# A state space layer and a windowed attention layer on one core: dividing the softmax numerators on GpSimd, and moving work across the border of the two layers

## The chip, the cores and the metric

The program runs on one core of a Trainium2 chip. The metric is the device time of one execution in microseconds (us), from the first to the last instruction of the core. The engines of the core are named as in its profile: PE (TensorE, matrix products and transposes; PEld is its weight load), DVE (VectorE), ACT (ScalarE), POOL (GpSimd) and SP (SyncE, which here only issues DMA transfers). All arithmetic is in fp32.

## The reference, cut to what matters

Two residual layers follow each other on `x` of shape (4, 384, 64, 64). Each is preceded by a group norm over 32 groups of 12 channels. Layer 0 is a state space layer (a scan over 4096 positions); the change touches only its surroundings. Layer 1 is attention of 12 heads of 32 channels over a 7 by 7 window around each pixel.

```python
def _L1_conv_ref(x, w_qkv, b_qkv, w_proj, b_proj, rel_bias):
    ...                                           # q, k, v: 1x1 products; edges of k and v repeated
    logits = jnp.stack([jnp.einsum('bnchw,bnchw->bnhw', q, k_pad[..., di:di + H, dj:dj + W])
                        for di in range(ws) for dj in range(ws)], axis=-1)
    logits = logits + rel_bias.reshape(nh, ws * ws)[None, :, None, None, :]
    attn = jax.nn.softmax(logits, axis=-1)
    v_win = ...                                   # the 49 shifted copies of v
    out = jnp.einsum('bnhwk,bnkchw->bnchw', attn, v_win).reshape(B, C, H, W)
    out = jnp.einsum('oc,bchw->bohw', w_proj, out) + b_proj[None, :, None, None]
    return out

x = x + _L0_conv_ref(_gn(x), ...)                 # state space layer
x = x + _L1_conv_ref(_gn(x), ...)                 # attention
```

## The kernel before

Layer 0 gives its instructions in the order in which the engines run them. In layer 1 the order on each engine is chosen when the program is built: an instruction may come before others that stand ahead of it in the code, once its inputs are there. Each engine then works through its own list strictly in that order, and waits where an input or a buffer is missing.

Layer 1 works on stripes of 8 rows of an image (32 stripes). A stripe has 4 blocks of 8 by 16 pixels, and a block has 3 groups of 4 heads. One group of one block is called a **step** here: 12 steps in a stripe, 384 in all. A step computes scores of 128 pixels against a common neighbourhood of 14 by 22 = 308 positions, with a bias table that masks what is outside of each pixel's own window.

```python
def scores(b, s, bl, m, blk):
    sg = w2.tile([P, 4, NK], F32, tag="sg", ...)             # 2 buffers
    mx = w2.tile([P, 4], F32, tag="mx", ...)
    for hh in range(4):
        lg = bank(ps_l, "lg")                                # 4 PSUM banks
        nc.tensor.matmul(lg[:, :NK], ...q..., ...k..., start=True, stop=True)       # L887
        nc.vector.tensor_tensor_reduce(                                            # L893
            sg[:, hh, :], lg[:, :NK], bias[:, 4 * m + hh, :], -1.0, BIG,
            ALU.add, ALU.min, mx[:, hh : hh + 1])
        act(sg[:, hh, :], sg[:, hh, :], AF.Exp, scale=-1.0, bias=mx[:, hh : hh + 1],
            accum_out=blk["sum"][:, 4 * m + hh : 4 * m + hh + 1])                   # L96
    return sg

def weighted(m, sg, blk):                     # numerators turned, so that positions are partitions
    ta = []
    for pair in range(2):
        pt = bank(ps_t, "pt")                                # 2 PSUM banks
        ...nc.tensor.transpose(pt[...], sg[...], ident)      # 4 of them, L912
        t = w2.tile([P, 4, P], F32, tag="ta", bufs=4)
        nc.vector.tensor_copy(...t..., pt[: KN[0], :])       # L917
        ta.append(t)
    pt = bank(ps_t, "pt")
    ...nc.tensor.transpose(pt[...], sg[:, hh, KOFF[2] :], ident)   # 4 of them, L923
    tb = w2.tile([P, 4, P], F32, tag="tb")
    nc.scalar.copy(...tb..., pt[: KN[2], :])                 # L927
    return ta, tb

def attended(m, ta, tb, blk):                 # L935: products with the window of v, 12 of them
    ...

def block_end(bl, blk, aT):                   # once in three steps
    rs = w2.tile([P, NH], F32, tag="rsum")
    nc.vector.reciprocal(rs, blk["sum"])                                           # L944
    rb = w2.tile([P, NH, HD], F32, tag="rb")
    nc.gpsimd.tensor_copy(rb, rs.unsqueeze(2).broadcast_to([P, NH, HD]))           # L946
    pr = bank(ps, "mm")                                      # the only bank of this pool
    for m in range(NJ):
        nc.tensor.transpose(pr[...], rb[...], ident)                               # L949
    rt = w2.tile([P, NJ, P], F32, tag="rt")
    nc.scalar.copy(..rt.., pr[:, : NJ * P])                                        # L954
    nc.vector.tensor_tensor(aT[...], blk["o"][...], ..rt.., ALU.mult)              # L955
```

The loop gives, in each step, the scores of this step, the product with v of the step before last, the transposes of the last step, and one part of `projected` (keys, values and queries of the next stripe) or of `stripe_end` (output projection of the last stripe). Both use the one bank of pool `ps`.

```python
for m in range(NJ):
    sg = scores(b, s, bl, m, blk)
    if turned is not None:
        attend()                              # attended(), and block_end() after the third group
    turned = None
    if pending is not None:
        pm, psg, pblk, *rest = pending
        turned = (pm, *weighted(pm, psg, pblk), pblk, *rest)
    pending = (m, sg, blk, bl, b, s, aT)
    if ends and next(ends[0], None) is None:
        ends.pop()
    elif not ends:
        next(ahead, None)                     # a part of projected(next stripe)
```

At the border of the layers, layer 1 first loads the bias table, then turns the channel statistics of all four images into group statistics (`group_stats`: eight small parts that depend on each other, with matrix products, DVE copies and ACT roots), and then projects the first stripe through the single bank of `ps`. The weights of layer 1 (`w_qkv`, `w_pj`) were loaded at the start of the program, and 18 small products (`pvb`) fold a bias there.

Of the kernel before, what the change touches and what calls it, by code (L numbers as in the profile page):

```python
# [8 lines left out]
F32 = mybir.dt.float32  # L9
AF = mybir.ActivationFunctionType  # L10
ALU = mybir.AluOpType
PSUM = bass.MemoryType.PSUM
DRAM = bass.MemoryType.DRAM

P = 128
C = 384
NJ = C // P
HW = 64
L = HW * HW
DI = 768  # L20
ND = DI // P
NS = 16
NG = 4
DTR = 24
KC = 4
NX = DTR + 2 * NS
T = 256
NCHUNK = L // T
# [4 lines left out]
NH = 12  # L33
# [15 lines left out]
def two_layers(  # L49
# [53 lines left out]
    small = ctx.enter_context(tc.tile_pool(name="small", bufs=2))  # L103
    dram = ctx.enter_context(tc.tile_pool(name="dram", bufs=2, space=DRAM))


# [44 lines left out]

    def load(shape, src, name):
        t = const.tile(shape, F32, name=name)
        nc.sync.dma_start(t, src)
        return t

    def column(src, n, name):
        return load([P, n], src.rearrange("(k p) -> p k", p=P), name)

# [5 lines left out]
    with nc.allow_non_contiguous_dma(reason="small vectors, one element per partition"):  # L165
        lnw = column(ln_w, NJ, "lnw")
        lnb = column(ln_b, NJ, "lnb")
        cvb = column(conv_b, ND, "cvb")
        dtb = column(dt_b, ND, "dtb")
        dsk = column(d_skip, ND, "dsk")  # L170
        qkb = column(qkv_b, 3 * NJ, "qkb")
        pjb = column(proj_b, NJ, "pjb")
    nega = load([P, ND, NS], a_log.rearrange("(k p) n -> p k n", p=P), "nega")
# [5 lines left out]

    dcv = const.tile([P, ND, KC, P], F32, name="dcv")  # L180
    for d in range(ND):
        for k in range(KC):
            nc.vector.tensor_scalar(dcv[:, d, k, :], ident, w_cv[:, d, k : k + 1], None, ALU.mult)
    dsd = const.tile([P, ND, P], F32, name="dsd")
    for d in range(ND):
        nc.vector.tensor_scalar(dsd[:, d, :], ident, dsk[:, d : d + 1], None, ALU.mult)
    binp = const.tile([P, 2 * ND], F32, name="binp")
    with tc.tile_pool(name="ps_fold", bufs=1, space=PSUM) as fps:
# [10 lines left out]


    w_qkv = const.tile([P, NJ, 3 * C], F32, name="w_qkv")
    nc.sync.dma_start(w_qkv, qkv_wT.rearrange("(k p) m -> p k m", p=P))
    w_pj = load([P, NJ, C], proj_wT.rearrange("(k p) m -> p k m", p=P), "w_pj")
    with tc.tile_pool(name="ps_vb", bufs=1, space=PSUM) as fps:
        pb0 = fps.tile([P, 512], F32, name="pvb")
        for m in range(NJ):
            for j in range(NJ):
                nc.tensor.matmul(
                    pb0[:, m : m + 1], w_pj[:, j, m * P : (m + 1) * P], qkb[:, 2 * NJ + j : 2 * NJ + j + 1],
                    start=(j == 0), stop=(j == NJ - 1),  # L210
                )
        nc.vector.tensor_tensor(pjb, pjb, pb0[:, :NJ], ALU.add)

    state = const.tile([P, ND, NS], F32, name="state")
    xb = const.tile([P, ND, KC - 1 + T], F32, name="xb")

# [65 lines left out]

    def layer0(x1s, mvs):

        with ExitStack() as es:
# [413 lines left out]
            for qi in range(RB):  # L699
                slot_of(3 + qi)(40, lambda qi=qi: biased(qi))  # L700

            def run(I, a=0, z=SLOTS):
                for slot in plan[I][a:z]:
                    for what in slot:
                        what()
# [33 lines left out]

    def layer1(x1s, mvs):  # L740
        scale = HD**-0.5
        with ExitStack() as es:
# [7 lines left out]
            bias = wt.tile([P, NH, NK], F32, name="bias")  # L750
            nc.sync.dma_start(bias.rearrange("p h k -> p (h k)"), bm)
            gms, vds = [], []
            for b in range(NB):
                gms.append(small.tile([P, NJ, 2], F32, tag="gm1", name=f"gm_b{b}", bufs=NB))
                for part in group_stats(mvs[b], gms[b], ps, f"b{b}"):
                    part()
                vds.append(dram.tile([WP, WP, C], F32, tag="vd", name=f"vd_{b}"))

            def bank(pool, tag):
                return pool.tile([P, 512], F32, tag=tag, name=f"{tag}_ps")  # L760

            def projected(b, s, h):

# [23 lines left out]
                for m in range(NJ):  # L787
                    for r0, r1 in ((0, PAD), (PAD, n)) if s == 0 else ((PAD, n),):
                        cols = (r1 - r0) * HW
                        pk = bank(ps, "mm")  # L790
                        for j in range(NJ):
                            nc.tensor.matmul(  # L792
                                pk[:, :cols], w_qkv[:, j, C + m * P : C + (m + 1) * P],
                                xn[:, j, r0:r1, :].rearrange("p r c -> p (r c)"),
                                start=(j == 0), stop=(j == NJ - 1),
                            )
                        act(
                            k[:, m, PAD + r0 : PAD + r1, PAD : PAD + HW],
                            pk[:, :cols].rearrange("p (r c) -> p r c", c=HW),
                            AF.Identity, bias=qkb[:, NJ + m : NJ + m + 1],  # L800
                        )
                    yield
# [18 lines left out]
                for r0 in range(old, n, 2):  # L821
                    rows = min(2, n - r0)
                    pv = bank(ps, "mm")
                    for j in range(NJ):
# [27 lines left out]
                for m in range(NJ):  # L852
                    pq = bank(ps, "mm")
                    for j in range(NJ):
# [12 lines left out]
            def window(b, s, bl):  # L867

                vw = w2.tile([P, 3, C], F32, tag="vw", name=f"vw_{b}_{s}_{bl}")
                r = RB * s  # L870
# [9 lines left out]
            def scores(b, s, bl, m, blk):  # L880

                sg = w2.tile([P, 4, NK], F32, tag="sg", name=f"sg_{b}_{s}_{bl}_{m}")
                mx = w2.tile([P, 4], F32, tag="mx", name=f"mx_{b}_{s}_{bl}_{m}")
                for hh in range(4):
# [16 lines left out]
                    )  # L901
                return sg

            def weighted(m, sg, blk):
# [36 lines left out]
            def block_end(bl, blk, aT):  # L941

                rs = w2.tile([P, NH], F32, tag="rsum", name="rsum")
                nc.vector.reciprocal(rs, blk["sum"])  # L944
                rb = w2.tile([P, NH, HD], F32, tag="rb", name="rb")
                nc.gpsimd.tensor_copy(rb, rs.unsqueeze(2).broadcast_to([P, NH, HD]))  # L946
                pr = bank(ps, "mm")
                for m in range(NJ):
                    nc.tensor.transpose(  # L949
                        pr[:, m * P : (m + 1) * P],  # L950
                        rb[:, 4 * m : 4 * m + 4, :].rearrange("p h e -> p (h e)"), ident,
                    )
                rt = w2.tile([P, NJ, P], F32, tag="rt", name="rt")
                nc.scalar.copy(rt.rearrange("p m q -> p (m q)"), pr[:, : NJ * P])  # L954
                nc.vector.tensor_tensor(  # L955
                    aT[:, :, :, bl * CB : (bl + 1) * CB],
                    blk["o"][:, : NJ * P].rearrange("p (m r c) -> p m r c", m=NJ, r=RB),
                    rt.rearrange("p m (r c) -> p m r c", r=RB), ALU.mult,
                )
# [21 lines left out]

            pending, turned, ends = None, None, []

# [11 lines left out]
            stripes = [{} for _ in todo]  # L995
            for _ in projected(*todo[0], stripes[0]):
                pass
            vw = window(*todo[0], 0)
            for n, (b, s) in enumerate(todo):
                ahead = iter(())  # L1000
                if n + 1 < len(todo):
                    stripes[n + 1]["before"] = stripes[n]["k"]
                    ahead = projected(*todo[n + 1], stripes[n + 1])
                aT = w2.tile([P, NJ, RB, HW], F32, tag="aT", name=f"aT_{b}_{s}", bufs=1)
                for bl in range(NBLK):
                    blk = {"q": stripes[n]["q"], "k": stripes[n]["k"], "v": vw}
                    blk["sum"] = w2.tile([P, NH], F32, tag="sum", name=f"sum_{b}_{s}_{bl}")
                    if bl + 1 < NBLK:
                        vw = window(b, s, bl + 1)
                    for m in range(NJ):  # L1010
# [3 lines left out]
                        turned = None  # L1014
                        if pending is not None:
                            pm, psg, pblk, *rest = pending
                            turned = (pm, *weighted(pm, psg, pblk), pblk, *rest)
                        pending = (m, sg, blk, bl, b, s, aT)
                        if ends and next(ends[0], None) is None:
# [7 lines left out]
            attend()  # L1027
            pm, psg, pblk, *rest = pending
            turned = (pm, *weighted(pm, psg, pblk), pblk, *rest)
            attend()  # L1030
            for _ in ends.pop():
# [3 lines left out]
    mvs = [small.tile([P, NJ, 2], F32, tag="mv1", name=f"mv1_{b}", bufs=NB) for b in range(NB)]  # L1035
    layer0(x1s, mvs)
    layer1(x1s, mvs)


# [44 lines left out]
```

## Time and profile before

| | us |
|---|---|
| time, median of 3 runs (9434.01 to 9439.41) | 9436.14 |
| span of the profiled execution | 9436.4 |
| last residual of layer 0 written by DVE (xo, L636) | 6809.3 |
| first scores of layer 1 (L887) | 6884.4 |
| first product with v (L935) | 6898.4 |
| PE busy of 1000 us, between 8000 and 9000 us | 934.5 |
| DVE, ACT, POOL busy in the same stretch | 574.1, 470.0, 33.6 |

The page of the profile lists busy times by engine, a picture of the span in 40 slices, the chain of work that ended last, and the costliest groups of instructions. A share of busy time over the whole span mixes the two layers, so the answers by stretch of time, the list of who waited for whom, and the timeline of single instructions are read beside it. In a line of the timeline, the number in square brackets is the idle time of that engine just before the instruction, with what ended it. A product in fp32 appears as two matrix records of the same line (PE L887: 8 records for 4 heads), a transpose as one.

### The profile page before, as it was taken

What the parts mean: (1) busy time and instruction counts of PE and PEld (TensorE: products, weight loads), DVE (VectorE), ACT (ScalarE), POOL (GpSimd) and SP (SyncE); (2) the same over time, 40 slices, a digit from 0 to 9 for tenths busy, and PEclk for the clock granted to TensorE, in tenths of its full rate; (3) what the DMA queues carried; (4) which work ended last, traced back from release to release, by engine and by line L of the source; (5) the groups of instructions that cost most, each with busy time, mean ns of one, the idle gap of its engine ahead of it and who ended that gap; (6) DMA issues with size and microseconds to landing.
All of it is one profiled execution on the core that took longest, in us unless ns stands there. A gap on an engine that the chain in (4) does not pass through costs nothing.

```text
span 9436.4 us, 139560 instructions
## 1 busy us (share of the span) xinstructions
PE 7804.9 (83%) x46266; PEld 5722.8 (61%) x46266; DVE 7485.8 (79%) x15348; ACT 5773.9 (61%) x13694; POOL 6104.2 (65%) x5271
## 2 busy tenths in 40 slices
PE   7877887788777877787788777877789999999999
PEld 5666666666666666666666666666545555555555
DVE  6888988898889888988898888888755555555555
ACT  5666666666766676666666766676444444444444
POOL 5888988898989898988889989998700000000000
PEclk8887888788878888888788888887699999999999
DMA  3111111111111111111111111111122222222222
GB/s 107 51 49 61 54 51 43 58 54 51 49 59 55 47 45 61 54 51 49 59 50 47 43 57 48 47 43 59 51 72 77 67 80 76 74 77 78 75 76 62
DMA packets 301912, 557.92 MB, mean 59 GB/s; under 512 B 61916, under 2 KB 185580, under 8 KB 301060
## 3 DMA queue, kind: packets, MB, share of 16 engines
q1 hardware_dynamic: 301188, 549.00, 18.4%
q8 instruction: 365, 5.98, 0.3%
q14 instruction: 359, 2.94, 0.1%
HBM read 446.33 MB, written 84.73 MB: 56 GB/s over the span
## 4 chain that ended last, share of the span: by engine, by line
PE 36%; DVE 28%; ACT 16%; POOL 10%; issue 9%; DMA 0%; SPq 0%; DVEq 0%; ACTq 0%; POOLq 0%
DVE hp L570 9%; DVE hs L570 8%; POOL db L550 5%; DVE hv L577 5%; PE mm_ps L628 5%; ACT da L96 4%; POOL hs L582 4%; PE y L590 3%; ACT sg L96 3%; PE mm_ps L393 3%; PE lg_ps L887 3%; PE mm_ps L969 3%; PE mm_ps L792 3%; PE mm_ps L855 3%; PE pt_ps L912 2%
## 5 line engine op out<-in xcount | busy, mean ns | idle before, releaser
L96 ACT ACTIVATE da<-dt,nega 128x256 f32<-128x256 f32 x6144 | 2922.8, 477 | 1416.8 <-DVE hs L570 972.3
L550 POOL TENSOR_TENSOR db<-dtx,B 128x1024 f32<-128x1024 f32 x1536 | 3620.9, 2357 | 30.1
L570 DVE TENSOR_TENSOR_SCAN hs<-da,state,db 128x256 f32<-128x256 f32 x2880 | 2118.6, 736 | 347.8 <-ACT da L96 347.8
L570 DVE TENSOR_TENSOR_SCAN hp<-da,state,db 128x256 f32<-128x256 f32 x2880 | 2153.8, 748 | 303.0 <-POOL state L581 192.9
L582 POOL TENSOR_TENSOR hs<-hs,C 128x512 f32<-128x512 f32 x1536 | 1952.2, 1271 | 123.2 <-POOL state L581 0.8
L590 PE MATMUL y<-ident,hv 128*128 128x128 f32 x6144 | 1192.0, 327 | 960.5 <-DVE hv L577 953.8
L590 PEld LDWEIGHTS y<-ident,hv 128*128 128x128 f32 x6144 | 850.5, 165 | 1409.5 <-DVE hv L577 1292.1
L96 ACT ACTIVATE sg<-sg,mx 128x308 f32<-128x308 f32 x1536 | 830.0, 541 | 890.1 <-DVE mx L893 889.8
L946 POOL COPY rb<-rsum 128x384 f32<-128x384 f32 x128 | 65.4, 511 | 2017.0 <-DVE rsum L944 1901.5
L590 PE MATMUL y<-ident,hs 128*128 128x128 f32 x6144 | 1156.4, 321 | 137.1 <-POOL hs L582 135.6
L393 PE MATMUL mm_ps<-xn,w_in 128*128 128x256 f32 x4608 | 1163.9, 404 | 2.0 <-DVE xn L369 2.0
L577 DVE TENSOR_TENSOR hv<-hp,C 128x512 f32<-128x512 f32 x1536 | 1044.3, 680 | 0.0
L590 PEld LDWEIGHTS y<-ident,hs 128*128 128x128 f32 x6144 | 901.8, 169 | 184.0 <-POOL hs L582 180.4
L393 PEld LDWEIGHTS mm_ps<-xn,w_in 128*128 128x128 f32 x4608 | 925.3, 207 | 133.3 <-issue 3.4
L893 DVE CUSTOM_DVE_ANT_0 sg<-lg_ps,bias 128x308 f32<-128x308 f32 x1536 | 650.4, 474 | 261.1 <-PE lg_ps L887 258.4
L400 PE MATMUL mm_ps<-xb,dcv 128*128 128x256 f32 x3072 | 716.9, 379 | 0.0
L581 POOL COPY state<-hs 128x2 f32<-128x2 f32 x1536 | 289.7, 189 | 523.6 <-DVE hs L570 461.9
L400 PEld LDWEIGHTS mm_ps<-xb,dcv 128*128 128x128 f32 x3072 | 567.6, 190 | 72.5
L500 PE MATMUL mm_ps<-xd,w_dt 24*128 24x256 f32 x768 | 335.4, 577 | 289.9 <-DVE yg L617 287.0
L628 PE MATMUL mm_ps<-yg,w_out 128*128 128x256 f32 x2304 | 520.9, 380 | 0.0
L917 DVE COPY ta<-pt_ps 110x512 f32<-110x512 f32 x768 | 495.4, 680 | 24.1 <-PE pt_ps L912 21.4
L927 ACT COPY tb<-pt_ps 88x512 f32<-88x512 f32 x384 | 223.1, 581 | 392.2 <-PE pt_ps L923 392.2
(139 smaller groups left out, 10832.0 us busy)
## 6 DMA issues: line engine op xcount, KB each, us to landing
B<-bcrows SPq DMA_DIRECT2D x256, 512.0 KB
C<-bcrows SPq DMA_DIRECT2D x256, 512.0 KB
vw<-vd SPq DMA_DIRECT2D x1792, 33.0 KB
xr<-x SPq DMA_DIRECT2D x28, 1056.0 KB
vd<-v SPq DMA_DIRECT2D x280, 96.0 KB
xi<-in_x_dram SPq DMA_DIRECT2D x64, 384.0 KB
x<-xo SPq DMA_DIRECT2D x64, 384.0 KB
o<-x SPq DMA_DIRECT2D x96, 256.0 KB
```

The costliest lines, as they stand in the source:

```text
L96: ins = nc.scalar.activation(o, i, func, **kw)
L393: nc.tensor.matmul(pb[:, k, :], w_in[:, j, m * P : (m + 1) * P], xn[:, j, :], start=(j == 0), stop=(j == NJ - 1),)
L400: nc.tensor.matmul(pb[:, k, :], dcv[:, d, c, :], xb[:, d, c : c + T], start=(c == 0), stop=(c == KC - 1),)
L500: nc.tensor.matmul(t["pb"][:, k, :], w_dt[:, (2 * q + k) * P : (2 * q + k + 1) * P], h["xd"][:DTR, :], start=True, stop=True,)
L550: nc.gpsimd.tensor_tensor(db, h["dtx"].unsqueeze(1).broadcast_to([P, NG, T]), h["bc"][g][0], ALU.mult)
L570: nc.vector.tensor_tensor_scan(to[:, k, :], da[:, k, :], db[:, 2 * half + k, :], state[:, d, n + k : n + k + 1] if I % NCHUNK else 0.0, AL ...
L577: nc.vector.tensor_tensor(hv, hp, ct[:, 0:2, :], ALU.mult)
L582: nc.gpsimd.tensor_tensor(hs, hs, ct[:, 2:4, :], ALU.mult)
L590: nc.tensor.matmul(y[:, half, :], t[:, k, half * P : (half + 1) * P], ident, is_transpose=True, start=(first and half == 0), stop=(last an ...
L628: nc.tensor.matmul(h["po", first][:, m - first, :], w_out[:, d, m * P : (m + 1) * P], h["yg"][d], start=(d == 0), stop=(d == ND - 1),)
L893: nc.vector.tensor_tensor_reduce(sg[:, hh, :], lg[:, :NK], bias[:, 4 * m + hh, :], -1.0, BIG, ALU.add, ALU.min, mx[:, hh : hh + 1],)
L917: nc.vector.tensor_copy(t[: KN[0], :, :].rearrange("p a q -> p (a q)"), pt[: KN[0], :])
```

## The change: what it does and what it is for

The division by the softmax sum moves. Before, a block was divided once, after the product with v: the reciprocals were spread to the channels, turned by PE through the bank that the projections also use, copied by ACT, and multiplied in by DVE. After, each step's numerators are divided in place by GpSimd before they are transposed, with a small reciprocal on DVE; the end of a block is a plain copy. For this, transposes now follow the scores by two steps in place of one, with more buffers (`sg`, `vw`, `sum`, `aT`). It is meant to take transposes, copies and their waits from PE, ACT and DVE, and to use an engine that has little to do in this layer.

At the border of the layers, the group statistics of the first three images are computed inside layer 0; the first stripe is projected through the four banks of the scores; the bias table is loaded after it. Tiles that only layer 0 uses are given back after it, and the attention weights are loaded at the border into the room that this leaves, with the 18 small products moved there too.

```diff
+    only0 = ctx.enter_context(ExitStack())
+    w0 = only0.enter_context(tc.tile_pool(name="w0", bufs=1))
...                                                     (layer 0's weights go to w0, not const)
-    w_qkv = const.tile([P, NJ, 3 * C], F32, name="w_qkv")
-    nc.sync.dma_start(w_qkv, qkv_wT.rearrange("(k p) m -> p k m", p=P))
-    w_pj = load([P, NJ, C], proj_wT.rearrange("(k p) m -> p k m", p=P), "w_pj")
...                                                     (18 products and an addition go with them)
+            for b in range(NB - 1):                     (in layer 0)
+                for n, part in enumerate(group_stats(mvs[b], gms1[b], ps, f"b{b}")):
+                    slot_of((b + 1) * NCHUNK)(SLOTS + 31 + 3 * n, part)
...
-            nc.sync.dma_start(bias.rearrange("p h k -> p (h k)"), bm)
-            gms, vds = [], []
-            for b in range(NB):
-                gms.append(small.tile([P, NJ, 2], F32, tag="gm1", name=f"gm_b{b}", bufs=NB))
-                for part in group_stats(mvs[b], gms[b], ps, f"b{b}"):
-                    part()
+            w_qkv = wt.tile([P, NJ, 3 * C], F32, name="w_qkv")
+            nc.sync.dma_start(w_qkv, qkv_wT.rearrange("(k p) m -> p k m", p=P))
+            w_pj = wt.tile([P, NJ, C], F32, name="w_pj")
+            nc.sync.dma_start(w_pj, proj_wT.rearrange("(k p) m -> p k m", p=P))
...                                                     (then the 18 products and the addition)
+            def normalised(m, sg, blk):
+                rs = w2.tile([P, 4], F32, tag="rsum", name="rsum")
+                nc.vector.reciprocal(rs, blk["sum"][:, 4 * m : 4 * m + 4])
+                for hh in range(4):
+                    nc.gpsimd.tensor_scalar(
+                        sg[:, hh, :], sg[:, hh, :], rs[:, hh : hh + 1], None, ALU.mult
+                    )
...
             def block_end(bl, blk, aT):
...                                                     (reciprocal, rb, transposes, rt removed)
-                nc.vector.tensor_tensor(
+                nc.vector.tensor_copy(
                     aT[:, :, :, bl * CB : (bl + 1) * CB],
                     blk["o"][:, : NJ * P].rearrange("p (m r c) -> p m r c", m=NJ, r=RB),
-                    rt.rearrange("p m (r c) -> p m r c", r=RB), ALU.mult,
                 )
...
-            for _ in projected(*todo[0], stripes[0]):
+            for _ in projected(*todo[0], stripes[0], ps_l, "lg"):
                 pass
+            nc.sync.dma_start(bias.rearrange("p h k -> p (h k)"), bm)
             vw = window(*todo[0], 0)
+            for part in group_stats(mvs[NB - 1], gms[NB - 1], ps, f"b{NB - 1}"):
+                part()
...
-                        if pending is not None:
-                            pm, psg, pblk, *rest = pending
+                        if pending:
+                            normalised(*pending[-1][:3])
+                        if len(pending) > 1:
+                            pm, psg, pblk, *rest = pending.pop(0)
                             turned = (pm, *weighted(pm, psg, pblk), pblk, *rest)
-                        pending = (m, sg, blk, bl, b, s, aT)
+                        pending.append((m, sg, blk, bl, b, s, aT))
```

## The prediction

> **What bounds the kernel now.** I read the busy times by stretch first, because the picture in slices shows two layers of different kinds. The columns are PE, PEld, DVE, ACT and POOL busy time with instruction counts, the clock, the DMA share and GB/s; the first row lies in layer 0, the second in layer 1.
>
> ```profile
> 100.00:6500.00 6400.00, 5076.97 (x24921) 4125.07 (x24920) 5705.30 (x10241) 4355.05 (x9544) 5738.08 (x4821) 0.82 0.16 52
> 8000.00:9000.00 1000.00, 934.54 (x7721) 520.42 (x7720) 574.08 (x1759) 470.03 (x1438) 33.63 (x78) 1.00 0.26 77
> ```
>
> Layer 0 keeps DVE and POOL at 90% each; the change hardly touches its loop. Layer 1, from 6884.4 to 9436.4 us (2552 us, 384 steps, 6.6 us each), is PE's: 93% busy, and GpSimd has 3% of work. So what counts is PE's own work there and the holes in it. Who PE waited for, between 6900 and 9400 us (total, times, longest):
>
> ```profile
> PE pt_ps L923 <- DVE ta L917: 84.0, 72, 1.6
> PE mm_ps L825 <- ACT rt L954: 35.9, 32, 1.4
> PE mm_ps L792 <- ACT rt L954: 30.1, 27, 1.1
> ```
>
> That is nearly all: 84 us on a transpose bank that DVE has not emptied, and 66 us on the one projection bank, which holds the turned reciprocals until ACT has copied them. The list for the other engines says why DVE is late:
>
> ```profile
> DVE rsum L944 <- ACT sg L96: 79.1, 65, 1.5
> ```
>
> 65 waits of the reciprocal for the last exponential of its own step, 1.22 us each, stand against 72 waits of PE. One such step in the timeline (the second row ends the scores' reductions):
>
> ```profile
> 8042.79 0.47 DVE L893 CUSTOM_DVE_ANT_0 sg<-lg_ps,bias 128x308 f32<-128x308 f32 x1
> ...
> 8043.79 0.54 ACT L96 ACTIVATE sg<-sg,mx 128x308 f32<-128x308 f32 x1
> ...
> 8044.52 0.23 DVE L944 RECIPROCAL rsum<-sum 128x12 f32<-128x12 f32 x1 [1.25 <-ACT sg L96]
> 8044.66 1.24 DVE L917 COPY ta<-pt_ps 110x512 f32<-110x512 f32 x2
> ...
> 8045.37 0.64 PE L923 MATMUL pt_ps<-ident,sg 128*88 128x128 f32 x4 [1.33 <-DVE ta L917]
> ```
>
> The reader is to see the order on DVE: the reciprocal is in front of the two bank copies, though the code has it two steps later. It was placed as soon as its sums were expected. DVE then stands still for the exponentials, the copies come 1.25 us late, and PE waits 1.33 us. Three steps beside each other, from first score reduction to first score reduction, size it: 8041.59 to 8048.05, with the reciprocal in front, is 6.46 us; 8048.05 to 8053.08, with neither, is 5.03 us; 8053.08 to 8059.94, with turned reciprocals and the wait for rt, is 6.86 us. A step with the reciprocal in front thus costs about 1.4 us more.
>
> The border of the layers: layer 0's last residual is done at 6809.3, the four chains of statistics end at 6835.3, the first scores start at 6884.4, so 75 us lie between.
>
> **What the Trainium skill says.** "GPSIMD Engine Reference", section 4.1 Engine selection, calls GpSimd about half as fast as DVE on two inputs and near line rate on one. The trace agrees: a two-input 128x512 product takes 1271 ns on POOL, a one-input copy of 128x384 511 ns. The same page and "PSUM — Partial Sum Buffer", section The four PSUM rules, keep GpSimd out of PSUM; the division is placed where the numerators lie in SBUF, so that is met. "SBUF — State Buffer", section Who interferes with whom, says that GpSimd and DVE share a port pair, and that a DVE instruction with at most one SBUF input outside its two-port modes does not collide. The frequent DVE instructions of layer 1 read PSUM and at most one SBUF tile, so I charge nothing; no run so far shows POOL busy beside them.
>
> **The change part by part.**
>
> *Removed from PE:* three transposes per block. A block's three take 0.48 us on the chain; 128 blocks make 61 us. *Removed waits:* the waits for rt, 35.9 + 30.1 + 1.1 (one on L855) = 67 us. If the reciprocals also stopped delaying the copies, 65 x 1.17 us (84.0 over 72) = 76 us more. All together 204 us; by steps it is a little more, since a stripe's periodic 79.4 us would become 72.
>
> *Added on POOL:* 4 x 384 multiplies of 128x308. From copies of 128x72 (258 ns) and 128x384 (511 ns), 0.81 ns per element, I estimate 450 ns, so 1.8 us per step of 6.6: it fits, and a step of slack is left before the transposes read it. Even at the two-input rate (128x1024 in 2357 ns and 128x512 in 1271 ns give 2.1 ns per element, 840 ns here) it would be 3.4 us.
>
> *Added on DVE:* 384 reciprocals in place of 128, some 0.2 us each, so 256 x 0.2 = 51 us on an engine with 43% free. By itself harmless. But **where** they stand is the question. Looking at each of the 128 blocks, I find the reciprocal in front of the copies in 65, nearly all in the last two blocks of a stripe (61 of 64), and behind them in the first two (60 of 64). In the last two blocks the order on PE is alike in all six steps: scores, product with v, eight transposes, two projections, four transposes, four projections. Only the third step of a block has had a reciprocal. Now every step has one, ready at the same moment relative to the copies. I therefore expect about six steps in twelve with the reciprocal in front, where two are now: four more in each of 32 stripes, 128 x 1.4 = 180 us given back.
>
> So attention's steady part: -61 (transposes) - 67 (rt) + 180 (reciprocals) = about +50. With n such steps in a stripe the sum is -128 + 32 x 1.4 x (n - 2): zero near n = 5, -220 at n = 0.
>
> *Border.* The three chains of 5.8 us leave PE's path at the border, 17 us; the fourth moves behind the projection. Their small parts in layer 0 cost a few us there at most. Four banks in place of one save the eviction waits in K (18.8 us from 6835.5 to 6854.3, of which some 4 are waits). But values then wait for their DMA issues: 42 issues of about 0.6 us on SP ran from 6857.8 to 6884.4, and the v tile has three buffers, so the queries can't come much sooner. w_qkv (1728 KB), w_pj and xr must now land at the border; the eight x loads (6 MB) at the start took about 20 us, so these 3.3 MB take some 11, and then 18 small products of 4 us in all follow. The first scores should come about 20 us earlier. At the end one more step drains alone, +3 us; at the start the folding leaves PE's path, -1.5 us. Together -20 us.
>
> Sum for the likeliest case: 9436 + 50 - 20 = about 9465.
>
> **The rivals.**
>
> 1. *The waits go away.* With a step of slack the reciprocals may be placed behind the copies, because transposes and projections keep other places when rt no longer uses the bank. For it: in half the blocks they are behind already, without a wait. Against it: the six alike steps. Time: 9436 - 220 - 20 = about 9200.
> 2. *Part of them.* Three or four steps in twelve: -128 + 32 x 1.4 x 1.5 = about -60, and -20 at the border: about 9355.
> 3. *GpSimd becomes the bound.* Needs 1.6 us per multiply; the copy and product rows speak against it. It would give 9700 or more. DVE's normalisation of the next stripe (three per stripe, 128x704 in 642 ns) takes less per element than a bank copy (512 in 680 ns) and may be in a two-port mode; its collisions would cost under 1 us a stripe.
> 4. *The loads at the border are late:* w_out is read until layer 0's last products, and if w_qkv lies in its room, nothing can start before about 6809. That takes back 10 to 20 us, and no more.
>
> **Range and chances.** The likeliest single case (about half) is 9430 to 9490; the case without waits (somewhat over a fifth) is 9170 to 9245; the rest lies between. The middle of the whole is about 9410. The range that leaves a tenth on each side is 9200 to 9490. Faster by over 2% means under 9247: 0.22. Slower by over 2% means over 9625, which only a slow GpSimd or waits in nearly all steps and at the border would give: 0.04. The rest: 0.74.
>
> **What would show it right or wrong.** POOL's multiplies of 128x308 at about 450 ns. No wait for rt left. The reciprocal's total wait for ACT's exponentials: about 32 x 6 x 1.2 = 230 us if I am right, near zero in rival 1; PE's wait at L923 for ta moves with it. First scores near 6865. The prediction is wrong at its core if the reciprocals stand behind the copies and PE is over 97% busy in the stretch from 8000 to 9000, or if POOL's multiplies, not ACT, hold the transposes.

## The result, and the profile after

The changed kernel takes **9405.67 us** (median, 9404.24 to 9415.21), the kernel before beside it 9435.64 us: a ratio of 0.997 [0.9953, 0.9987], so 30 us or 0.3% less. 9410 had been predicted.

The two rows by stretch come first again (the columns are those of the prediction). Of the kernel after:

```profile
100.00:6500.00 6400.00, 5074.38 (x24984) 4127.57 (x24984) 5713.10 (x10258) 4354.40 (x9545) 5737.66 (x4821) 0.82 0.16 52
8000.00:9000.00 1000.00, 913.60 (x7694) 504.77 (x7686) 586.43 (x1881) 458.46 (x1411) 640.52 (x636) 1.00 0.27 78
```

Layer 0's busy times hardly change. In layer 1 PE has fallen from 934.5 to 913.6 busy us in 1000. It has less to do, and it waits more. POOL has gone from 34 to 641 us. Whom PE waited for, between 6850 and 9370 us (total, times, longest):

```profile
PE pt_ps L932 <- DVE ta L926: 174.3, 235, 1.7
...
PE pt_ps L921 <- POOL sg L909: 2.4, 3, 1.2
```

The waits for rt (66 us on the two lines shown before) are gone, and no reciprocal is turned any more. But the wait for a transpose bank that DVE has not emptied has doubled, from 84.0 to 174.3 us. PE waits 2.4 us for POOL's multiplies, so they are not the bound. The list of all engines names the same releaser as before:

```profile
DVE rsum L907 <- ACT sg L96: 159.3, 138, 1.3
```

138 waits of a reciprocal for the last exponential of its own step, where there were 65. One such step in the timeline of the kernel after:

```profile
8113.45 0.47 DVE L894 CUSTOM_DVE_ANT_0 sg<-lg_ps,bias 128x308 f32<-128x308 f32 x1
...
8114.45 0.54 ACT L96 ACTIVATE sg<-sg,mx 128x308 f32<-128x308 f32 x1
...
8115.18 0.18 DVE L907 RECIPROCAL rsum<-sum 128x4 f32<-128x4 f32 x1 [1.25 <-ACT sg L96]
...
8115.28 1.29 DVE L926 COPY ta<-pt_ps 110x512 f32<-110x512 f32 x2
8115.52 4.15 POOL L909 TENSOR_SCALAR sg<-sg,rsum 128x308 f32<-128x308 f32 x4 [1.12 <-DVE rsum L907]
...
8116.02 0.64 PE L932 MATMUL pt_ps<-ident,sg 128*88 128x128 f32 x4 [1.34 <-DVE ta L926]
```

It is the picture of before with another line number: the reciprocal stands in front of the bank copies, DVE is still for 1.25 us, and PE misses the bank for 1.34 us. In a steady stripe this is so in 4 of the 12 steps, the seventh, eighth, tenth and eleventh. From first score reduction to first score reduction they last 7.2, 6.9, 6.5 and 6.4 us. A steady stripe went from 79.5 to 78.1 us. POOL's new row in the list of costliest groups (busy us, mean ns | idle us before):

```profile
L909 POOL TENSOR_SCALAR sg<-sg,rsum 128x308 f32<-128x308 f32 x1536 | 1603.9, 1064 | 917.1 <-DVE rsum L907 771.1
```

A multiply took 1064 ns, not 450. Where the time went, from the two profiled spans (9436.4 and 9402.5 us, 34 us apart): layer 0 ends 0.6 us later, the first scores start 23.4 us earlier (6884.4 to 6861.0), and the first stripe then takes 7.1 us longer (72.6 to 79.7 us), so its successor starts 16.3 us earlier. The remaining 17.6 us come from all 31 stripes after it, a small part of the 204 us of work and waits that stood there.

### The profile page after: what moved, and what is told of

Read it like the earlier page. It is cut to its first block, busy times and chain, and to the rows that moved or that the text cites. A ratio compares the mean times of both kernels' runs of the same rounds, so it can differ in the third digit from the quotient of the medians.

```text
span 9402.5 us, 141121 instructions
## 1 busy us (share of the span) xinstructions
PE 7733.7 (82%) x45882; PEld 5668.8 (60%) x45882; DVE 7512.0 (80%) x15604; ACT 5726.1 (61%) x13566; POOL 7641.1 (81%) x6679
## 5 line engine op out<-in xcount | busy, mean ns | idle before, releaser
L909 POOL TENSOR_SCALAR sg<-sg,rsum 128x308 f32<-128x308 f32 x1536 | 1603.9, 1064 | 917.1 <-DVE rsum L907 771.1
L616 PE MATMUL mm_ps<-yg,w_out 128*128 128x256 f32 x2304 | 518.8, 379 | 0.0
```

The source lines that it names most:

```text
L616: nc.tensor.matmul(h["po", first][:, m - first, :], w_out[:, d, m * P : (m + 1) * P], h["yg"][d], start=(d == 0), stop=(d == ND - 1),)
L909: nc.gpsimd.tensor_scalar(sg[:, hh, :], sg[:, hh, :], rs[:, hh : hh + 1], None, ALU.mult)
```

## The experiments

**The theory:** the order on DVE takes back what the division brings; a reciprocal in front of the copies stalls DVE, and PE with it. **Rivals:** POOL's multiplies, over twice as long as estimated, hold the transposes or disturb DVE; or the border brought the gain and the attention nothing. The kernel before, run beside these kernels, took 9433.4 to 9434.3 us (medians). The expectations name the runs by labels: e1 and e2 are experiments 1 and 2, e5 is the first run of 5, e8 the first of 7, and e10 and e11 the two of 8 with the normalisation on ACT.

**1. The reciprocal behind the copies.** An order edge is added: it keeps the reciprocal from being placed ahead of the second bank copy of the same step. Both are DVE's, so it adds no wait on a semaphore.

```diff
-                nc.vector.reciprocal(rs, blk["sum"][:, 4 * m : 4 * m + 4])
+                inv = nc.vector.reciprocal(rs, blk["sum"][:, 4 * m : 4 * m + 4])
+                if copies:
+                    behind(inv, copies[-1])        # order only, same engine
...
-                    nc.vector.tensor_copy(         # ta
+                    copied = nc.vector.tensor_copy(
...
+                copies.append(copied.ins.name)
```

> The kernel after, with one edge of order added: the reciprocal of a step's sums may stand on DVE only behind the two bank copies (ta) of that step. No work is added or taken away. Theory (order on DVE): the 159.3 us in which reciprocals wait for ACT's exponentials fall to under 10, PE's wait at the last four transposes for ta (174.3 us, 235 times) falls to under 50, and the time comes down by 130 to 175 us, to 9230 to 9275. Rival (GpSimd): its multiplies take 1064 ns each, 4.26 us of a 6.6 us step, and it is their lateness that the rest is arranged around; then a reciprocal that comes later makes transposes wait for POOL, and the time stays at 9390 or rises.

Measured: 9252.91 us, 0.9807 [0.9794, 0.9821] of the kernel before, 153 us less than the change. Its waits between 6900 and 9200 us:

```profile
PE pt_ps L947 <- DVE ta L940: 45.4, 111, 0.8
...
DVE rsum L919 <- ACT sg L96: 0.7, 2, 0.4
```

A step of it in the timeline; the last reduction, then at once the copies, and the reciprocal behind them without a wait:

```profile
8110.25 0.47 DVE L906 CUSTOM_DVE_ANT_0 sg<-lg_ps,bias 128x308 f32<-128x308 f32 x1
...
8110.65 1.28 DVE L940 COPY ta<-pt_ps 110x512 f32<-110x512 f32 x2
...
8111.54 0.60 PE L947 MATMUL pt_ps<-ident,sg 128*88 128x128 f32 x4
...
8111.98 0.18 DVE L919 RECIPROCAL rsum<-sum 128x4 f32<-128x4 f32 x1
```

In a steady stripe the four steps named above now last 6.5, 5.6, 5.0 and 5.0 us. The other eight are as long as before, so the stripe falls from 78.1 to 73.3 us. The multiplies are as long as in the change (1061 ns), yet PE's stretch from 8000 to 9000 is now full:

```profile
8000.00:9000.00 1000.00, 964.18 (x8164) 537.78 (x8163) 624.52 (x1997) 484.04 (x1489) 676.04 (x673) 1.00 0.28 84
```

The theory holds; GpSimd as the bound falls.

**2. The same edge in the kernel before.** There a block's reciprocal may not come ahead of a bank copy of the step after its own.

```diff
-                nc.vector.reciprocal(rs, blk["sum"])
+                inv = nc.vector.reciprocal(rs, blk["sum"])
+                if len(copies) > 1:
+                    behind(inv, copies[-2])
```

> The kernel before, with the same edge: the reciprocal of a block's sums stands behind the two bank copies of the block's third step. Theory (order on DVE): its 79.1 us of waits for ACT go, PE's 84.0 us of waits for ta fall to about 10, and the time falls by 75 to 95 us to about 9350, under that of the kernel after. Rival: PE only moves its waiting to the bank of the projections (rt, 66 us), since reciprocals, their spreading and their transposes all come later; then the time falls by under 30 us.

Measured: 9350.02 us, 0.991 [0.9897, 0.9924]: 84 us less. The waits between 6900 and 9200 us:

```profile
PE mm_ps L825 <- ACT rt L969: 34.8, 31, 1.4
...
PE mm_ps L792 <- ACT rt L969: 29.0, 26, 1.1
...
PE pt_ps L936 <- DVE ta L929: 4.0, 10, 0.9
```

Only the bank wait is gone; the waits for rt stay. In a steady stripe only the two steps with the stall change, by 1.43 us each. One edge in the kernel before brings more than the whole change.

**3 and 4. The two halves of the change.** The first has the division on GpSimd with the border of before; the second the new border with the attention of before.

```diff
 (division alone: the border of the kernel before)
-            w_qkv = wt.tile(...); w_pj = wt.tile(...)          (loaded at the border)
+    w_qkv = const.tile(...); w_pj = load(..., const)           (at the start, with the 18 products)
-            for b in range(NB - 1): ... slot_of(...)(..., part)
+            for part in group_stats(mvs[b], gms[b], ps, f"b{b}"): part()
-            for _ in projected(*todo[0], stripes[0], ps_l, "lg"):
+            for _ in projected(*todo[0], stripes[0]):
```

> The division on GpSimd with its buffers alone; the border of the layers as before (weights loaded at the start, all four chains of statistics before the first projection, first stripe through one bank, bias table loaded first). Theory: the steady part of attention is nearly even, since two thirds more reciprocals in front of the copies give back what the removed transposes (61 us) and rt waits (67 us) bring; 9415 to 9435. Rival: the division carries the gain of 30 us and the border nothing; then 9405.

> The border changes alone (statistics of three images inside layer 0, first stripe through four banks, bias after it, weights loaded at the border); the division at the end of a block as before. Theory: first scores some 23 us earlier than before, and the time follows: about 9412. Rival: the first products with v are bound by the DMA issues of the values on SP and come no earlier, so that most of the 23 us is waited away in the first stripe: 9425 to 9440.

Measured: division alone 9398.16 us, 0.9961 [0.9948, 0.9975]; border alone 9427.86 us, 0.9992 [0.9984, 1.0]. The first is a miss: the rival was right that the division carries the whole gain, and it is even 7.5 us better without the new border. The intervals of 9398.16 and of the change (9405.67) overlap, but their single runs do not (9396.54 to 9401.45 and 9404.24 to 9415.21). The border alone is within its rival's 9425 to 9440, and its gain is at the edge of the noise. Its layer 0 ends 7.0 us later than before (6816.3), its first scores still come at 6867.5, but the first product with v comes at 6898.5, as before: what was won is waited away.

**5. One GpSimd product for four multiplies,** on top of the edge (1) and, in a second run, on the change as it is:

```diff
-                for hh in range(4):
-                    nc.gpsimd.tensor_scalar(
-                        sg[:, hh, :], sg[:, hh, :], rs[:, hh : hh + 1], None, ALU.mult
-                    )
+                nc.gpsimd.tensor_tensor(
+                    sg, sg, rs.unsqueeze(2).broadcast_to([P, 4, NK]), ALU.mult
+                )
```

> The kernel after with the edge of order, and the four multiplies of a step on GpSimd put as one two-input product of 128x1232 against the reciprocals spread by a stride of zero. From the two-input rows (2.12 ns per element) one such product is 2.8 us, against 4 x 1.064 = 4.26 us. Theory (order on DVE, POOL not the bound): POOL's busy time falls by about 500 us and the time stays with the kernel that has the edge alone, 9253, within 15 us. Rival (GpSimd's lateness still costs): under 9230.

> The kernel after, without the edge, with the one product of 128x1232 on GpSimd. Theory (order on DVE): reciprocals still stand ahead of the bank copies in about a third of the steps, PE's wait for ta stays at 140 to 190 us, the time at 9390 to 9420. Rival (GpSimd): a third less work on POOL brings more than 25 us: under 9380.

Measured: 9301.58 us, 0.9859 [0.9846, 0.9873], with the edge, and 9465.58 us, 1.0036 [1.0023, 1.0048], without. Both expectations missed. POOL is done sooner (2244 ns for the four, in place of 4 x 1061), and yet the kernels are 49 and 60 us slower. The row that moved stands on DVE: the normalisation of the next stripe (`xn`, 128x704). Between 6900 and 9200 us, in the kernel before and in the first of these two (count | busy us, mean ns):

```profile
L779 DVE TENSOR_SCALAR xn<-xr,gm_b 128x704 f32<-128x704 f32 x78 | 49.8, 641 | 0.0
L780 DVE TENSOR_SCALAR xn<-xr,gm_b 128x704 f32<-128x704 f32 x78 | 92.0, 1185 | 0.0
```

It took 740 ns in the kernel after, and 724 in that of experiment 1.

**6. The factor a constant.** The division is left out: every multiply is by 1.0 and waits for no reciprocal.

```diff
-                        sg[:, hh, :], sg[:, hh, :], rs[:, hh : hh + 1], None, ALU.mult
+                        sg[:, hh, :], sg[:, hh, :], 1.0, None, ALU.mult
```

> The kernel after with the edge, in which the multiplies on GpSimd take a constant 1.0 in place of the reciprocal per partition: the division is left out, so the output is not the reference's, and the multiplies no longer wait for DVE's reciprocal. It measures what the per-partition operand costs: if it is what makes 1064 ns out of the 450 ns estimated from copies, the multiply takes 430 to 550 ns; if a multiply costs that in any form, it stays at 1000 to 1070. The time stays at about 9253 either way if POOL is not the bound.

Measured: 994 ns for a multiply, 9273.13 us, 0.983 [0.9812, 0.9848]. So the column of factors is not what makes it long (1061 to 994 ns). The time does not fall below that of 1, with its division: it is 20 us higher, where no change was expected. Layer 0 is some 4 us longer here, and a steady stripe takes 73.7 us against 73.3; why was not traced.

**7. The edge and the division with the old border, and then four banks for the first stripe.**

```diff
 (division alone + the edge of 1; and then, in the second run)
-            for _ in projected(*todo[0], stripes[0]):
+            for _ in projected(*todo[0], stripes[0], ps_l, "lg"):
```

> The division on GpSimd with the edge of order, and the border of the layers as before the change. Theory: the edge brings here what it brought with the new border (152 us), 9398 - 152 = 9246, and the new border brings nothing on top, so the two are within 15 us of each other. Rival: the new border's 17 us between the end of layer 0 and the second stripe count once the order is right; then 9265 to 9275.

> The kernel of e8 (division on GpSimd, edge of order, old border) with one piece of the new border: the first stripe is projected through the four banks of the scores. Theory: the longer first stripes of the new border (stripes 2 to 4 together 13.8 us longer in e1 than in e8) come with scores that start before the values are written out, so this piece alone brings them: first scores some 4 to 8 us earlier, time within 8 us of e8's 9249. Rival: they come from the loads and statistics at the border; then the four banks bring 4 to 10 us: about 9241.

Measured: 9248.61 us, 0.9803 [0.9789, 0.9816], and with four banks 9257.83 us, 0.9813 [0.98, 0.9827], so 9 us more. The first met its expectation. The second misses its own by a little (9 us for 8, and first scores 11 us earlier for 4 to 8); its rival, a gain, is wrong. The copies of the first stripe's v rows on DVE show why. With one bank:

```profile
6858.66 0.56 DVE L832 COPY v<-mm_ps 128x384 f32<-128x384 f32 x1 [2.30 <-PE mm_ps L825]
6864.40 0.56 DVE L832 COPY v<-mm_ps 128x384 f32<-128x384 f32 x1 [5.18 <-DMA vd<-v]
6868.26 0.56 DVE L832 COPY v<-mm_ps 128x384 f32<-128x384 f32 x1 [3.30 <-PE mm_ps L825]
6873.01 0.55 DVE L832 COPY v<-mm_ps 64x384 f32<-64x384 f32 x1 [4.20 <-PE mm_ps L825]
```

With four banks PE's v products (L825) were through by 6857.7, but:

```profile
6851.80 0.56 DVE L832 COPY v<-lg_ps 128x384 f32<-128x384 f32 x1 [1.38 <-PE lg_ps L825]
6872.63 0.56 DVE L832 COPY v<-lg_ps 128x384 f32<-128x384 f32 x1
6883.84 0.55 DVE L832 COPY v<-lg_ps 128x384 f32<-128x384 f32 x1
6895.20 0.54 DVE L832 COPY v<-lg_ps 64x384 f32<-64x384 f32 x1
```

The last three copies show no wait: they stand on DVE behind queries, normalisations and score reductions. The loads of the windows of v need all rows, and began at 6897.6 in place of 6880.2. So the first scores come 11 us earlier (6868.8 for 6880.1), the first product with v 14 us later (6910.1 for 6896.6), and the first stripe takes 76.5 us in place of 63.0. The three stripes behind it are 14 us longer together as well, as in 1; why is not shown.

**8. The normalisation off DVE.** It goes to ACT, as a scale and a bias, with the division by four multiplies or by one product; and one product with the normalisation on DVE, to close the square.

```diff
-                    nc.vector.tensor_scalar(
-                        xn[:, j, :n, :], xr[:, j, :n, :], gm[:, j, 0:1], gm[:, j, 1:2],
-                        ALU.subtract, ALU.mult,
+                    act(
+                        xn[:, j, :n, :], xr[:, j, :n, :], AF.Identity,
+                        scale=gm[:, j, 1:2], bias=gbs1[b][:, j, :],      # -mean * scale
```

> The kernel of e8 with the normalisation of the next stripe (128x704, three per stripe, L779) on ACT in place of DVE, four multiplies per step on GpSimd. With e11 it asks whether GpSimd and DVE hold each other up at these instructions. Theory: with four short multiplies they hardly do (mean 724 ns for 641 ns before), so the move brings under 15 us: 9235 to 9255.

> The kernel of e10 with one product of 128x1232 per step on GpSimd. Theory (the long GpSimd instruction holds up DVE's normalisation, 1185 ns in e5): with no normalisation on DVE, one product costs no more than four multiplies, so within 15 us of e10. Rival (another order of instructions, which the builder finds for the one product, costs the 49 us of e5): 40 us or more above e10.

> The kernel of e8 with one product of 128x1232 per step on GpSimd and the normalisation on DVE, as in e5: the fourth of the square of e8, e10 and e11. Theory: the 49 us that e5 lay above e1 come again, 9290 to 9305, and the normalisation takes over 1100 ns on DVE.

| us (all with the edge and the old border) | four multiplies | one product | difference |
|---|---|---|---|
| `xn` on DVE | 9248.61 | 9298.01, 0.9856 [0.9842, 0.9869] | +49.4 |
| `xn` on ACT | 9230.27, 0.9785 [0.9772, 0.9799] | 9229.29, 0.9782 [0.9769, 0.9796] | -1.0 |

The one product costs 49 us only where DVE normalises. In a steady stripe it changes the second step alone, in which the normalisations stand (7.0 us with four multiplies, 8.5 or 10.1 with one product); the other eleven are as long, so a different order of instructions is not the cause. The timeline of that kernel (one product, `xn` on DVE) shows one meeting:

```profile
8097.31 3.10 DVE L779 TENSOR_SCALAR xn<-xr,gm_b 128x704 f32<-128x704 f32 x2
...
8097.53 2.48 POOL L921 TENSOR_TENSOR sg<-sg,rsum 128x1232 f32<-128x1232 f32 x1 [26.22 <-DVE rsum L918]
...
8100.46 1.12 PE L792 MATMUL mm_ps<-xn,w_qkv 128*128 128x512 f32 x2 [1.32 <-DVE xn L779]
```

Two normalisations take 3.10 us where two of the kernel before take 1.28. They end 0.40 us after POOL's product, and PE waits 1.32 us. "SBUF — State Buffer" of the Trainium skill, section Who interferes with whom, says that a tensor_scalar of DVE can run in a two-port mode, and that such an instruction and one of GpSimd exclude each other for the whole instruction. The runs agree. In this kernel, of the 90 normalisations between 6900 and 9200 us, the 53 that met no POOL instruction took 637 ns in the median, the 37 that met one 2477 ns. And by kernels: the longer the GpSimd instruction, the longer the `xn` row (740 ns in the change, whose multiplies take 1.06 us; 1217 ns here, beside products of some 2.2 us), and on ACT (966 ns with either) nothing is lost. With four multiplies the move brings 18 us, where under 15 had been expected. The two kernels with `xn` on ACT are the fastest of all.

## Why the prediction was right or wrong

**The mechanism** was right: what bounds the attention after the change is the place of the reciprocal on DVE, not the division on GpSimd. The waits for rt and the turned reciprocals went as expected; the reciprocals' waits came to 159 us, where about 230 had been expected. The sum of the attention, however, had the wrong sign. The runs allow each term of its attention sum to be measured:

| term | predicted | measured | from |
|---|---|---|---|
| division itself (transposes and rt) | -128 | -101 | edge on the kernel before (2) to edge on the division alone (7): 9350.02 to 9248.61 |
| stalls there before | -90 (65 x 1.4) | -84 | kernel before to 2 |
| stalls after | +269 (192 x 1.4) | +150 | division alone with the edge (7) to without (3): 9248.61 to 9398.16 |
| sum | +50 | -36 | division alone: 9398.16 |

**The step that was mis-sized** is "about six steps in twelve with the reciprocal in front". It is four: of the six steps of each stripe's second half that were taken as alike, the two that end a block, the ninth and the twelfth, have the reciprocal behind the copies. In these the block end's plain copy (`aT`) stands on DVE between the last score reduction and the bank copies. In the kernel before, the block end stood a step earlier (the second, fifth, eighth and eleventh); as the products with v now follow a step later, it has moved to the third, sixth, ninth and twelfth. That the copy is what keeps the reciprocal behind is read from this order; no run moved it. (On PE, too, two of the six differed in the kernel before: in the eighth and the eleventh four projections, not two, stood before the last transposes.) The price of 1.4 us a step was right in three of the four (1.3, 1.4 and 1.4 us, from the steps with the edge and without); in the seventh step it is 0.7. With four steps in place of six, the prediction's own formula gives -128 + 32 x 1.4 x 2 = -38, and -36 was measured. That is closer than its terms deserve: the division brought 27 us less than the 128 counted, and the stalls cost some 30 less than four steps at 1.4 would.

**Where the division fell short.** With the edge (7) PE still waits 47.2 us for ta between 6900 and 9200 us, where the kernel before with its edge (2) waits 4.0. By steps, 15.2 us of it stand in the second step, behind the normalisations that meet POOL. They are gone with these on ACT (8), where 31.3 us remain. "Under 1 us a stripe" had been written for them and left out of the sum. The other 32.0 us stand in the sixth, ninth and twelfth step, behind the block end's copy. In the kernel of 7:

```profile
7880.53 0.55 DVE L965 COPY aT<-pv_ps 128x384 f32<-128x384 f32 x1
...
7881.00 1.28 DVE L939 COPY ta<-pt_ps 110x512 f32<-110x512 f32 x2
...
7881.74 0.64 PE L946 MATMUL pt_ps<-ident,sg 128*88 128x128 f32 x4 [0.36 <-DVE ta L939]
```

The prediction names no cost for the copy, which replaces a multiply as long (0.56 us); but in its new place PE waits behind it. The two waits together are more than the 27 us; the term is not taken apart further.

**POOL's multiply** at 450 ns was wrong by more than two. The copies' slope did not carry over to a multiply. It did no harm: four take 4.2 us of a step of 5.5, and the transposes come a step later. With the normalisation on ACT, a product that is done 2.0 us sooner in each step changed the time by 1.0 us (8).

**The border** was to bring 20 us. First scores at 6861 met the 6865 expected, but the -20 did not come: the border alone brings some 6 us, on top of the division it costs 7.5 (9398.16 to 9405.67), and with the edge 4 (9248.61 to 9252.91). Two things were missed. The end of the first stripe hangs on the last v row, its DMA issues and its window loads, not on the first scores; in the kernel after:

```profile
6843.97 0.56 DVE L833 COPY v<-lg_ps 128x384 f32<-128x384 f32 x1 [1.38 <-PE lg_ps L826]
6864.79 0.56 DVE L833 COPY v<-lg_ps 128x384 f32<-128x384 f32 x1
6876.00 0.55 DVE L833 COPY v<-lg_ps 128x384 f32<-128x384 f32 x1
6885.93 0.54 DVE L833 COPY v<-lg_ps 64x384 f32<-64x384 f32 x1
```

The rows are copied as late after their products as with four banks in 7, and the first product with v starts at 6903.9, 5.5 us later than before. And the statistics in layer 0 cost more than "a few us at most": from the first input product to the end of the last residual, the six kernels with them (the change, the border alone, 1, both of 5, and 6) take 6750.9 to 6755.7 us, the eight without (the kernel before, 2, the division alone, and all of 7 and 8) 6740.8 to 6747.7. The means are some 9 us apart. No run has the statistics alone, but they are the only work that the new border adds in that stretch. The profile of the change shows less of it (its layer 0 ends 0.6 us later than before): it began 2.6 us earlier, and is the shortest of the six, as that of the kernel before is the longest of the eight. Rival 4 was half right; these lines of the kernel after show the late loads:

```profile
6809.92 0.43 DVE L624 TENSOR_TENSOR xo<-mm_ps,xi 128x256 f32<-128x256 f32 x1 [1.90 <-PE mm_ps L616]
6810.05 0.38 SPq L745 DMA_DIRECT2D w_qkv<-in_qkv_wT_dram  x1
...
6819.70 3.97 PE L752 MATMUL pvb<-qkb,w_pj 128*128 128x1 f32 x18 [1.59 <-DMA w_pj<-in_proj_wT_dram]
...
6824.71 13.41 PE L793 MATMUL lg_ps<-xn,w_qkv 128*128 128x192 f32 x36 [1.04 <-DVE xn L780]
```

The load waited for layer 0's last products (L616) and was issued only then, and PE begins its first projection at 6824.7, 10.8 us earlier than the 6835.5 of before, where 17 us of chains had been taken away: some 6 us are taken back, not 10 to 20.

**The number** fits better than its parts, and that 9410 came within 5 us is luck. It was the middle of several cases and none of them; the likeliest, 9465, was 59 us too high: 86 from the attention, less 27 from the border. Rival 2, with three or four steps, had the count right and the time, 9355, too low by 50, 27 of it again the border's. Rival 1 ("about 9200") is what the edge makes of the kernel: 9252.91.

## What to carry to other kernels

Where the order on an engine is chosen at build time, look for small instructions that wait at the head of a strictly ordered list for another engine's last result, ahead of work that is ready; one order edge was worth 153 us after the change and 84 before it, more than the rewriting. When a change shifts work by a step, look at what the shifted work now stands in front of. Before work is moved to an idle engine, look at which of its neighbour's instructions share its port, and prefer several short instructions to a long one there. An earlier start counts only if the last input of that stretch, here the last v row and its loads, comes earlier too.

## What the runs showed of the hardware that was not expected

- A GpSimd multiply of 128x308 in place takes 1064 ns with a column of factors and 994 with a constant, 3.2 to 3.5 ns an element, where a copy to 128x384 (the spread reciprocals of the kernel before) takes 511 ns, 1.3 an element, and a product with a broadcast factor 2244 ns for 128x1232, 1.8 an element. "GPSIMD Engine Reference" of the Trainium skill, section 4.1 Engine selection, expects one input to run nearer to line rate than two. The copy agrees; this multiply does not, as it is slower per element than the two-input product.
- The same division done 2.0 us sooner in each step (4 x 1061 to 2244 ns) made the kernel 49 us slower, through a DVE instruction of which there are only about three in a stripe, and which grew from 724 to 1217 ns (641 beside a nearly idle GpSimd, in the kernel before).
